# Writing the biases of a four-layer graph kernel into PSUM banks instead of adding them by products

## The chip, the cores and the metric

The kernel runs on one core of one Trainium2 chip. TensorE multiplies and writes only to PSUM, which has eight banks of 512 float32 values in each of 128 partitions. VectorE (DVE in the profile) and ScalarE (ACT) read and write PSUM and SBUF, GpSimd (POOL) works on SBUF, and SyncE (SP) issues the transfers. The metric is the device time in microseconds (us) of one execution. Each engine takes its instructions in the order in which they were written to its queue, and waits on semaphores for the others.

## What is computed

Thirty-two graphs of 512 nodes with 128 features go through four layers. Each layer is preceded by a layer norm and a ReLU, and its result is added to the input. With `h = relu(layernorm(x))`:

```
layer 0: v, q, k = relu(h W + b)              three products, each with a bias
         x += softmax(mask(q k^T, adj)) v
layer 1: dyn = conv1d(last 128 nodes of h) + conv_b
         lw  = lstm(dyn)                      128 steps; all 32 graphs in one batch
                 z = xt w_ih^T + b_ih + hprev w_hh^T + b_hh
         x += sigmoid((A_norm h) lw)          A_norm = D^-1/2 (adj + I) D^-1/2
layer 2: n0 = h; for i in 0..3:
           n(i+1) = tanh([src_agg, self, dst_agg] wu + bu)
           src, dst, self = nodes ws + bs, nodes wd + bd, nodes wn + bn
         x += n4
layer 3: x += prelu(adj (h W^T) + bias)
```

The adjacency is symmetric with a full diagonal. The kernel uses this: it works on one matrix per graph, folds the two aggregations of layer 2 into one, and checks the symmetry as it goes, with a general kernel as the fallback.

## The kernel before

The function `symmetric` doesn't issue instructions as it goes. It collects operations in a `Plan`: each has one or more engines on which it may run, with an estimated duration for each, a rank (lower is more urgent), the buffers it reads and writes, and a function that issues its instructions. `Plan.run` then lays all operations out as a list scheduler would, chooses between ScalarE and VectorE where both are allowed, and calls the issuing functions in order of planned start. A tile framework below it allots the buffers, places the semaphores, and may still change the order on an engine: an instruction whose operands or buffer are not there yet in its own reckoning is passed by one that can go.

There are four groups of operations by rank:

- `pass_1(b)` for each graph b: load x and the last 128 columns of adj, layer norm, transpose (`ln_t`, tile f_xt), the products for keys and queries (f_pq) and values (f_pv), attention for the last 128 nodes (f_sl, f_pol), and the convolution (f_pd) into `seq`. Keys, queries and values go to DRAM.
- `lstm()`: 128 serial steps, rank below 1000, which makes them urgent. A bank `f_z` holds the four gates of four steps for all 32 graphs. At the first of the four the bias (four products of 4 rows, L1069) and the input part (four products, L1073) are written into it, and each step then adds four state products of 32 columns (L1079). A step goes on with a tanh on ScalarE (L1083), three VectorE instructions (L1090 to L1092), a tanh (L1099) and a VectorE product (L1100) which writes `seq` for the next.
- `pass_2(b)`, planned beside the LSTM: attention for the other 384 nodes. It has four score products (f_s, L1120), exponentials and masks, twelve value products (f_po, L1130), the update of x and its statistics.
- `rest(b, end)`: layers 1 to 3. It squares adj with row sums (f_ar), normalises, aggregates (f_pg, L1199), transposes the LSTM output (f_plw, L1206; this waits for the LSTM's last step), makes the gates (f_pl, L1213), checks symmetry (f_aT, L1229), and runs the four sub-layers of layer 2. Each of these has f_py (L1253), a split of f_py into high and low halves by `split` (ScalarE L1147, VectorE L1148), the aggregation into f_pa (L1262), a scaling of f_pa on VectorE (L1265), the own part (L1269) and a tanh (L1273). Layer 3 is f_pf (L1291) and f_pg3 (L1302; the profile drops the 3 and shows f_pg).

Biases that lie along the columns of a bank are added on TensorE. `bias_row` splits a bias row into a high and a low float32r half with four VectorE instructions (`in_parts`), and `add_bias` multiplies a matrix of ones by them as the first product of the bank:

```python
    def add_bias(dst, k, n=NT):
        nc.tensor.matmul(dst, ones_r, bparts[:, k, :].unsqueeze(1).to_broadcast([P, n, P]), start=True, stop=False,
                         skip_group_check=True)
```

This is L838; it is called for f_pv (32 times), f_py (128) and f_pg3 (64). The eight banks are one tag, "mm", of a pool with eight buffers:

```python
    ps = ctx.enter_context(tc.tile_pool(name="f_ps", bufs=BUFS["mm"], space=bass.MemoryType.PSUM))
    def bank(name, shape=(P, 512)):
        return plan.cell(ps, "mm", shape, FP, name)
```

The plan only counts how many are free; which buffer a tile gets is left to the framework.

Of the kernel before, what the change touches and what calls it, by code (L numbers as in the profile page):

```python
# [486 lines left out]
BR_V, BR_3, N_BR = 4, 5, 6  # L487
# [4 lines left out]
class Cell:  # L492


    def __init__(self, pool, tag, shape, dtype, name):
        self.pool, self.tag, self.shape, self.dtype, self.name = pool, tag, shape, dtype, name
        self.real = None
        self.left = 0
        self.free_at = 0.0
        self.parts = {}  # L500

    @property
    def t(self):
        if self.real is None:
            self.real = self.pool.tile(list(self.shape), self.dtype, tag=self.tag, name=self.name)
        return self.real
# [6 lines left out]
class Plan:  # L513
# [4 lines left out]

    HOP, HOP_PE, HOP_URGENT, URGENT = 0.25, 1.2, 0.14, 1000

    def __init__(self, bufs, fifo):
        self.ops = []
        self.bufs = bufs
        self.made = {}
        self.fifo = {t: [] for t in fifo}

    def cell(self, pool, tag, shape, dtype, name):
        c = Cell(pool, tag, shape, dtype, name)
        if tag in self.fifo:
            self.fifo[tag].append(c)  # L530
        return c
# [34 lines left out]
    def run(self):  # L566
# [16 lines left out]
        slots = {t: [0.0] * n for t, n in self.bufs.items()}  # L583
        turn = {t: 0 for t in self.fifo}
        seen = set()
# [40 lines left out]
        while done < len(ops):  # L626
# [33 lines left out]
            for c in o.cells:  # L660
                if c not in seen:
                    seen.add(c)
                    slots[c.tag].remove(min(slots[c.tag]))
# [4 lines left out]
                if c.left == 0:  # L668
                    slots[c.tag].append(c.free_at)
            for n in o.next:  # L670
# [11 lines left out]
def symmetric(ctx, tc, x, adj, weights, cols, rows, lstm_b, prelu_a, out, fail):  # L682
# [25 lines left out]
    ps = ctx.enter_context(tc.tile_pool(name="f_ps", bufs=BUFS["mm"], space=bass.MemoryType.PSUM))  # L708
# [7 lines left out]
    plan = Plan(BUFS, ("ar", "x", "inv", "n0", "n1", "n2", "n3", "a"))  # L716
# [14 lines left out]
    def bank(name, shape=(P, 512)):  # L731
        return plan.cell(ps, "mm", shape, FP, name)
# [33 lines left out]

    def evict(rank, n, dst, src, r, w, relu=False, scale=None):
# [19 lines left out]
    ones_r = const.tile([P, P], FR, name="f_ones_r")  # L787
    nc.vector.memset(f32(ones_r), 1.0)
# [7 lines left out]
    bparts = const.tile([P, N_BR, P], FR, name="f_bparts")  # L796
    lbp = const.tile([4, 4, P], FR, name="f_lbp")
# [10 lines left out]
    lb = const.tile([4, 4, P], FP, name="f_lb")  # L808
    nc.scalar.dma_start(lb[0:2], lstm_b)
    nc.scalar.dma_start(lb[2:4], lstm_b)  # L810
# [4 lines left out]
    mask2 = const.tile([4, 2], FP, name="f_mask2")  # L815
    nc.vector.tensor_add(mask2[:, 0:1], ident[0:4, 0:1], ident[0:4, 1:2])
    nc.vector.tensor_add(mask2[:, 1:2], ident[0:4, 2:3], ident[0:4, 3:4])
    biases = plan.fixed(bparts)
# [4 lines left out]
    def in_parts(rank, n, m, dst, src, masks, r, wr, name):  # L823
        hi = new("gs", (n, m), f"f_bhi_{name}", FR)
        lo = new("gs", (n, m), f"f_blo_{name}")

        def fn():
            nc.vector.tensor_copy(hi.t, src())
            nc.vector.tensor_sub(lo.t, src(), f32(hi.t))
            nc.vector.tensor_scalar_mul(lo.t, lo.t, masks[1])  # L830
            nc.vector.scalar_tensor_tensor(dst, f32(hi.t), masks[0], lo.t, OP.mult, OP.add)
        DVE(rank, 1.2, fn, r, [hi, lo] + wr)

    def bias_row(rank, k, row, r):
        in_parts(rank, P, P, bparts[:, k, :], row, (ident[:, 0:1], ident[:, 1:2]), r, [(biases, k)], k)

    def add_bias(dst, k, n=NT):
        nc.tensor.matmul(dst, ones_r, bparts[:, k, :].unsqueeze(1).to_broadcast([P, n, P]), start=True, stop=False,  # L838
                         skip_group_check=True)
# [5 lines left out]
    bias_row(HEAD, BR_3, lambda: rowb.t[:, R_L3, :], [rowb])  # L845
# [3 lines left out]
    def halves():  # L849
        for q in range(4):  # L850
            half = 1.0 if q == 2 else 0.5
            nc.gpsimd.tensor_scalar_mul(w[:, W_HH + q, :], w[:, W_HH + q, :], 0.5 * half)
            if q != 2:
                nc.gpsimd.tensor_scalar_mul(w[:, W_IH + q, :], w[:, W_IH + q, :], half)
                nc.gpsimd.tensor_scalar_mul(lb[:, q, :], lb[:, q, :], half)
    lbs = plan.fixed(lb)
    POOL(FOLD, 5.0, halves, [], [lbs])
    in_parts(FOLD, 4, 4 * P, flat(lbp), lambda: flat(lb), (mask2[:, 0:1], mask2[:, 1:2]), [lbs], [], "lb")
# [4 lines left out]
    def fold(i):  # L863
# [7 lines left out]
        for c in range(L2_CHUNKS[i]):  # L871
            tp = bank(f"f_wT_{i}_{c}", (P, 3, P))
# [7 lines left out]
            pw = bank(f"f_pw_{i}_{c}", (P, 2, P))  # L880
# [7 lines left out]
        bt_ps = bank(f"f_bT_{i}", (P, 3, P))  # L888
# [7 lines left out]
        pb = bank(f"f_pb_{i}", (P, P))  # L896
# [6 lines left out]
        pc = bank(f"f_pc_{i}", (P, 2))  # L903
# [52 lines left out]
    def ln_t(rank, xn, tag, name):  # L956
# [3 lines left out]
        def fn():  # L960
            for t in range(NT):
                nc.tensor.transpose(tp.t[:, t, :], xn.t[:, t, :], ident)
        PE(rank, 4 * T_TR, fn, [xn], [tp])
        hT = new(tag, (P, N), f"f_hT_{name}")
        evict(rank, N, lambda: hT.t[:, :], lambda: flat(tp.t), [tp], [hT], relu=True)
        return hT
# [6 lines left out]
    def pass_1(b):  # L973
# [6 lines left out]
        hT = ln_t(R, xn, "n0", f"a{b}")  # L980
# [11 lines left out]
        pv = bank(f"f_pv_{b}", (P, NT, P))  # L992

        def values():
            add_bias(pv.t, BR_V)
# [3 lines left out]
        PE(R, t_r(N) + 4 * t_mm(P), values, [hT, (biases, BR_V)], [pv])  # L999
# [12 lines left out]
        def scores():  # L1012
            for t in range(NT):
                nc.tensor.matmul(s.t[:, t, :], kq.t[:, 0, bass.ts(t, P)], kq.t[:, 1, NR:], start=True, stop=True)
# [4 lines left out]
        po = bank(f"f_pol_{b}", (P, P + 1))  # L1019
# [24 lines left out]
        pd = bank(f"f_pd_{b}", (P, P))  # L1044
# [11 lines left out]
    def lstm():  # L1056
# [4 lines left out]
        for t in range(T):  # L1061
            R = t
            k = t % MANY
            if k == 0:
                z = bank(f"f_z_{t}", (P, MANY, 4, B))

                def biases_in(z=z):
# [354 lines left out]
```

## Time and profile before

| | |
|---|---|
| median of 3 runs | 1642.4 us |
| lowest, highest | 1637.87, 1642.55 us |
| the profiled execution | 1644.95 us |
| its span, first to last instruction | 1642.8 us |
| mean granted TensorE clock | 0.972 |
| memory read, written | 117.26 MB, 39.91 MB |

A row of a group shows line, engine, operation, output and inputs, shapes and count; then busy time in us and the mean of one in ns; then the idle time of the engine before them and what ended it. TensorE's records overlap, since a product is recorded until its end while the next has begun: the distance from start to start says what one takes of the engine. A float32 product has two records, a float32r product one. The chain of waits is followed back from the last instruction, and gives start, length and what ran.

### The profile page before, as it was taken

The page shows a single profiled execution, that of the slowest core. Times are in us where ns is not written, and L with a number is a line of the kernel's source. Part 1 is how long each engine was busy: PE and PEld are TensorE (multiplying, and loading weights), DVE is VectorE, ACT ScalarE, POOL GpSimd, SP SyncE. Part 2 cuts the span into 40 slices and gives each one's busy share as a digit, 9 for nine tenths or more (in the row PEclk, how much of TensorE's full clock was granted, in tenths as well). Part 3 has the DMA queues.
Part 4 walks back from the last instruction along what each step waited for, and adds up shares of the span by engine and source line. Part 5 has one row for each costly group of instructions (what it writes and reads, how often), then busy time and mean ns, then how long its engine had stood idle before and what let it go on. Part 6 is the DMA issues. An engine that isn't in the chain of part 4 may idle for free.

```text
span 1642.8 us, 26595 instructions
## 1 busy us (share of the span) xinstructions
PE 1541.6 (94%) x9565; PEld 1253.9 (76%) x9565; DVE 938.4 (57%) x3322; ACT 715.9 (44%) x1700; POOL 322.6 (20%) x624
## 2 busy tenths in 40 slices
PE   4998899999999996999999999999999999999995
PEld 3776678888888885777878887787887787788774
DVE  4665555545554455646746656547656656656543
ACT  3555453323333334645534545435444545454431
POOL 3333331111111112212212212112111212211100
PEclk9999999999999998999999999999999999999997
DMA  7555567454555453101201212112211121111000
GB/s 242 182 187 172 192 203 248 136 165 139 148 152 167 138 147 108 61 33 54 95 14 46 71 39 78 39 39 76 67 39 44 48 65 52 65 39 36 17 13 16
DMA packets 135733, 158.98 MB, mean 97 GB/s; under 512 B 7588, under 2 KB 101924, under 8 KB 135592
## 3 DMA queue, kind: packets, MB, share of 16 engines
q1 hardware_dynamic: 134720, 155.41, 30.1%
q8 instruction: 77, 1.26, 0.3%
q10 hardware_dynamic: 872, 1.78, 0.3%
q14 instruction: 64, 0.52, 0.1%
HBM read 117.26 MB, written 39.91 MB: 96 GB/s over the span
## 4 chain that ended last, share of the span: by engine, by line
PE 42%; DVE 7%; POOL 4%; ACT 4%; DMA 1%; issue 1%; POOLq 0%; ACTq 0%
PE f_pa L1262 11%; PE f_pa L1269 9%; PE f_py L1253 9%; PE f_pg L1302 3%; PE f_pg L1199 2%; ACT f_ar L1163 2%; POOL f_dinv L1173 1%; PE f_pf L1291 1%; DMA f_a<-in_adj_dram 1%; PE f_py L838 1%; PE f_pl L1213 1%; PE f_aT L1229 1%; DVE f_junk L1231 1%; POOL f_rs_c L929 1%; DVE f_pa L1265 1%
## 5 line engine op out<-in xcount | busy, mean ns | idle before, releaser
L1262 PE MATMUL f_pa<-f_ar,f_y 128*128 128x512 f32 x1024 | 272.8, 410 | 5.7 <-DVE f_y L1148 3.0
L1262 PEld LDWEIGHTS f_pa<-f_ar,f_y 128*128 128x128 f32 x1024 | 187.0, 189 | 57.1 <-issue 10.7
L1253 PE MATMUL f_py<-f_wf,f_n 128*128 128x128 f32 x1280 | 174.5, 275 | 1.4 <-ACT f_n L1273 1.3
L1253 PEld LDWEIGHTS f_py<-f_wf,f_n 128*128 128x128 f32 x1280 | 165.2, 192 | 12.9 <-issue 4.3
L1269 PE MATMUL f_pa<-f_n,f_wf 128*128 128x512 f32 x320 | 155.6, 603 | 6.3 <-DVE f_pa L1265 6.2
L1079 PEld LDWEIGHTS f_z<-f_seq,f_w 128*128 128x128 f32 x1016 | 130.9, 200 | 30.7 <-DVE f_seq L1100 26.1
L1079 PE MATMUL f_z<-f_seq,f_w 128*128 128x32 f32 x1016 | 137.6, 280 | 5.5 <-DVE f_seq L1100 3.7
L1273 ACT ACTIVATE f_n<-f_pa,f_bcol 128x512 f32<-128x512 f32 x128 | 87.2, 683 | 107.9 <-PE f_pa L1269 107.8
L1148 DVE TENSOR_TENSOR f_y<-f_py,f_y 128x512 fp32r<-128x512 f32 x128 | 87.2, 685 | 77.0 <-ACT f_y L1147 76.5
L1265 DVE TENSOR_TENSOR f_pa<-f_pa,f_inv 128x512 f32<-128x512 f32 x128 | 88.1, 693 | 57.6 <-PE f_pa L1262 57.4
L1147 ACT CAST f_y<-f_py 128x512 fp32r<-128x512 f32 x128 | 73.6, 580 | 107.1 <-PE f_py L1253 106.5
L1130 PE MATMUL f_po<-f_v,f_e 128*128 128x129 f32 x768 | 119.4, 297 | 0.0
L1130 PEld LDWEIGHTS f_po<-f_v,f_e 128*128 128x128 f32 x768 | 106.9, 207 | 9.0
L940 ACT ACTIVATE f_xn_c<-f_x,f_sh_c,f_rs_c 128x128 f32<-128x128 f32 x127 | 57.0, 489 | 108.7 <-DVE f_sh_c L945 108.4
L1120 PE MATMUL f_s<-f_kq 128*128 128x384 f32 x256 | 103.2, 516 | 0.0
L1083 ACT ACTIVATE f_th<-f_z 128x128 f32<-128x128 f32 x128 | 35.5, 278 | 143.7 <-PE f_z L1079 138.3
L1269 PEld LDWEIGHTS f_pa<-f_n,f_wf 128*128 128x128 f32 x320 | 56.6, 192 | 49.3 <-issue 38.1
L1090 DVE SCALAR_TENSOR_TENSOR f_cu<-f_th,f_c 128x32 f32<-128x32 f32 x127 | 24.4, 192 | 120.9 <-ACT f_th L1083 120.0
L1231 DVE SCALAR_TENSOR_TENSOR f_junk<-f_a,f_aT 128x512 bf16<-128x512 f32 x128 | 86.4, 675 | 4.4 <-PE f_aT L1229 2.4
L1253 PE MATMUL f_py<-f_wf,f_hT_c 128*128 128x128 f32 x512 | 84.4, 277 | 0.7 <-ACT f_hT_c L770 0.7
L1163 ACT ACTIVATE f_ar<-f_a 128x512 fp32r<-128x512 f32 x128 | 79.2, 623 | 6.6 <-DMA f_a<-in_adj_dram 6.6
L1123 ACT ACTIVATE f_e<-f_s 128x384 f32<-128x384 f32 x128 | 62.7, 490 | 38.3 <-PE f_s L1120 36.8
(184 smaller groups left out, 3036.4 us busy)
## 6 DMA issues: line engine op xcount, KB each, us to landing
f_a<-in_adj_dram SPq DMA_DIRECT2D x32, 1024.0 KB, 5.3
f_a<-in_adj_dram SPq DMA_DIRECT2D x32, 768.0 KB, 5.6
f_dkq<-f_kq SPq DMA_DIRECT2D x32, 448.0 KB, 3.7
f_kq<-f_dkq SPq DMA_DIRECT2D x32, 448.0 KB, 4.0
f_dv<-f_v SPq DMA_DIRECT2D x32, 258.0 KB, 3.8
f_v<-f_dv SPq DMA_DIRECT2D x32, 258.0 KB, 2.7
f_x<-in_x_dram SPq DMA_DIRECT2D x32, 256.0 KB, 3.5
f_al<-in_adj_dram SPq DMA_DIRECT2D x32, 256.0 KB, 3.0
```

Of the source, the lines that this page charges most:

```text
L1079: nc.tensor.matmul(z.t[:, k, q, :], w[:, W_HH + q, :], seq[:, t - 1, :], start=False, stop=True, skip_group_check=True)
L1120: PE(R, t_mm(NR), lambda s=s, j=j: nc.tensor.matmul(s.t, kq.t[:, bass.ts(j, P)], kq.t[:, N:], start=True, stop=True), [kq], [s])
L1130: nc.tensor.matmul(po.t[:, t, :], es[j].t[:, bass.ts(t, P)], v.t[:, j, :], start=(j == 0), stop=(j == NT - 1))
L1147: ACT(rank, t_act(N), lambda: nc.scalar.copy(parts.t[:, :, 0, :], src.t), [src], [(parts, 0)])
L1148: DVE(rank, t_dve(N), lambda: nc.vector.tensor_sub(parts.t[:, :, 1, :], src.t, f32(parts.t[:, :, 0, :])), [src, (parts, 0)], [(parts, 1)])
L1163: ACT(R, 0.62, lambda t=t: nc.scalar.activation(ar.t[:, t, :], a.t[:, t, :], AF.Square, accum_out=deg.t[:, t : t + 1]), [a], [(ar, t), (de ...
L1231: DVE(R + 2, 0.7, lambda tp=tp, j=j: nc.vector.scalar_tensor_tensor(junk, a.t[:, j, :], 1.0, flat(tp.t), OP.mult, OP.not_equal, accum_out= ...
L1253: nc.tensor.matmul(py.t[:, j, :], nodes[n].t[:, bass.ts(j, P)], wf[:, W_F[i] + c, 0, :], start=False, stop=(c == nch - 1), skip_group_chec ...
L1262: nc.tensor.matmul(pa.t, parts.t[:, j, k, :], ar.t[:, j, :], start=(k == 0 and j == 0), stop=(k == 1 and j == NT - 1))
L1265: DVE(R, t_dve(N), lambda pa=pa: nc.vector.tensor_mul(pa.t, pa.t, inv_row.t), [inv_row], [pa])
L1269: nc.tensor.matmul(pa.t, wf[:, W_F[i] + c, 1, :], nodes[n].t, start=False, stop=(c == nch - 1), skip_group_check=True)
L1273: ACT(R, 0.5, lambda pa=pa, n=n, i=i: nc.scalar.activation(n.t, pa.t, AF.Tanh, bias=bcol[:, i : i + 1]), [pa], [n])
```

## The change

- No bias is added by a product any more. A bank that takes a bias is declared `filled`, and a new operation `fill` copies the bias row, repeated, into the whole bank, on ScalarE or VectorE as the plan chooses. All products then run with `start=False` and are added to it. For f_z the row `lb_row` holds the four gate biases for all graphs; for f_pg3 it has the bias in the high half's columns and zeros in the low half's.
- Each fill has an operation after which it may start: for f_py the scaling of f_pa of the sub-layer before (or the transpose of the nodes), for f_pv and f_pg3 the transpose before, for f_z the step that was formerly given to the bias products.
- Whether a product adds to what lies in a bank or replaces it depends on marks that earlier products left there. The plan keeps `marked` for each bank: set by a tile declared `whole`, whose products cover the bank under a single start, and cleared by others. `place` picks the bank: among the free ones one whose mark suits the tile, else the longest free. If a fill gets an unmarked bank, a product of zeros over the whole bank is issued first (L859 of the new kernel).
- To leave a bank marked, the four-tile products and transposes now start only at their first tile.
- The pool has one buffer, and the plan's choice is the tag: "mm0" to "mm7".
- The bias rows are copied as they are, instead of being split; the two LSTM biases are transposed together by one product (f_pb8), added, scaled by GpSimd's `halves`, and spread into `lb_row`.

```diff
-    def add_bias(dst, k, n=NT):
-        nc.tensor.matmul(dst, ones_r, bparts[:, k, :].unsqueeze(1).to_broadcast([P, n, P]), start=True, stop=False,
-                         skip_group_check=True)
+    def fill(rank, dst, src, r, c, after):
+
+        def mark():
+            if not c.marked:
+                nc.tensor.matmul(c.t, ident_b, marks, start=True, stop=True)
+
+        def act():
+            mark()
+            nc.scalar.copy(dst(), src)
+
+        def dve():
+            mark()
+            nc.vector.tensor_copy(dst(), src)
+        return plan.op({"ACT": (t_act(N), act), "DVE": (t_dve(N), dve)}, rank, r, [c], after)
...
+        def place(c, s):
+
+            now = [x for x in unused if x[0] <= s + 1e-9] or [min(unused)]
+            at = min(now, key=lambda x: (marked[x[1]] != c.filled, x))
+            unused.remove(at)
+            c.place = at[1]
+            c.marked = marked[c.place]
+            self.sealed += c.filled and not c.marked
+            marked[c.place] = c.whole
+            return at[0]
...
-            self.real = self.pool.tile(list(self.shape), self.dtype, tag=self.tag, name=self.name)
+            tag = self.tag if self.place is None else f"{self.tag}{self.place}"
+            self.real = self.pool.tile(list(self.shape), self.dtype, tag=tag, name=self.name)
...
-    ps = ctx.enter_context(tc.tile_pool(name="f_ps", bufs=BUFS["mm"], space=bass.MemoryType.PSUM))
+    ps = ctx.enter_context(tc.tile_pool(name="f_ps", bufs=1, space=bass.MemoryType.PSUM))
...
-    def bank(name, shape=(P, 512)):
-        return plan.cell(ps, "mm", shape, FP, name)
+    def bank(name, shape=(P, 512), whole=True, filled=False):
+        return plan.cell(ps, "mm", shape, FP, name, whole, filled)
...
+    def turn_tiles(dst, src):
+
+        for t in range(NT):
+            nc.tensor.matmul(dst[:, t, :], src(t), ident, start=(t == 0), stop=True, is_transpose=True, skip_group_check=True)
...
-                z = bank(f"f_z_{t}", (P, MANY, 4, B))
-
-                def biases_in(z=z):
-                    for q in range(4):
-                        nc.tensor.matmul(z.t[:, :, q, :], lbp[:, q, :], ones_r[:4, : MANY * B], start=(q == 0), stop=False,
-                                         skip_group_check=True)
-                PE(R + 2_000, 4 * t_r(P), biases_in, [], [z], after=conv_ops + steps[t - MANY - 1 : t - MANY])
+                z = bank(f"f_z_{t}", (P, MANY, 4, B), filled=True)
+
+                fill(R + 2_000, lambda z=z: z.t.rearrange("p k q b -> p k (q b)"),
+                     lb_row.unsqueeze(1).to_broadcast([P, MANY, 4 * B]), [lbrs], z, conv_ops + steps[t - MANY - 1 : t - MANY])
...
-            py = bank(f"f_py_{b}_{i}", (P, NT, P))
+            py = bank(f"f_py_{b}_{i}", (P, NT, P), filled=True)
+            fill(R, lambda py=py: py.t, bias(i), [(biases, i)], py, [before])
 
             def sent(py=py, i=i, nch=nch):
-                add_bias(py.t, i)
...
-            PE(R, t_r(N) + 4 * nch * t_mm(P), sent, [nodes[n] for n in CHUNKS[i]], [py])
+            PE(R, 4 * nch * t_mm(P), sent, [nodes[n] for n in CHUNKS[i]], [py])
...
-            DVE(R, t_dve(N), lambda pa=pa: nc.vector.tensor_mul(pa.t, pa.t, inv_row.t), [inv_row], [pa])
+            before = DVE(R, t_dve(N), lambda pa=pa: nc.vector.tensor_mul(pa.t, pa.t, inv_row.t), [inv_row], [pa])
...
-            p3 = bank(f"f_pg3_{b}_{k}", (P, 2, 2, P))
+            p3 = bank(f"f_pg3_{b}_{k}", (P, 2, 2, P), filled=True)
+            fill(R, lambda p3=p3: p3.t, bias_3.unsqueeze(1).to_broadcast([P, 2, 2, P]), [b3s], p3, [turned])
```

## Prediction

> **What bounds the kernel now.** I read the page's busy times and slices first, then windows by stage, then the groups kept apart by shape, then two stretches of the timeline.
>
> ```profile
> PE 1541.6 (94%) x9565; PEld 1253.9 (76%) x9565; DVE 938.4 (57%) x3322; ACT 715.9 (44%) x1700; POOL 322.6 (20%) x624
> ...
> 100.00:250.00 150.00, 133.21 (x863) 106.89 (x862) 84.61 (x397) 75.82 (x141) 51.94 (x143) 0.99 0.58 192
> 340.00:640.00 300.00, 287.39 (x1872) 244.52 (x1872) 156.72 (x753) 100.17 (x315) 49.41 (x86) 0.93 0.51 151
> 640.00:800.00 160.00, 150.58 (x908) 121.47 (x908) 99.66 (x294) 80.91 (x192) 31.98 (x53) 0.96 0.18 57
> 800.00:1000.00 200.00, 199.13 (x1231) 161.19 (x1230) 121.87 (x347) 97.83 (x228) 36.06 (x59) 1.00 0.15 49
> ```
>
> Window lines give PE, PEld, DVE, ACT and POOL busy time, then granted clock, DMA share and GB/s. There are three stages: pass 1 (to about 260 us, PE 89% busy in its middle), the LSTM with pass 2 beside it (to 629), and the rest (to the end, PE 97 to 99% busy once it runs). So the rest is bound by TensorE's throughput, and what leaves TensorE there should leave the time. The LSTM stage differs: it is a serial chain, and the timeline shows its period.
>
> ```profile
> 452.56 1.08 PE L1079 MATMUL f_z<-f_seq,f_w 128*128 128x32 f32 x8
> 455.11 1.08 PE L1079 MATMUL f_z<-f_seq,f_w 128*128 128x32 f32 x8
> ...
> 318.00:322.00 4.00, 4.00 (x24) 4.00 (x23) 0.68 (x4) 0.51 (x2) 0.00 (x0) 0.57 0.00 0
> ...
> 320.39 1.75 PE L1079 MATMUL f_z<-f_seq,f_w 128*128 128x32 f32 x8
> ```
>
> An undisturbed step takes 2.55 us (455.11 less 452.56): some 1 us of state products, the remainder ScalarE and VectorE, during which TensorE has 1.6 us for pass 2. At 318 the clock falls to 0.57 and the same eight records take 1.75 us: there TensorE is busy, but with short 32-column products.
>
> **What the skill says.** The Trainium skill, page "PSUM — Partial Sum Buffer", section "The four PSUM rules": VectorE and ScalarE writes leave the has_written bits alone, and a matmul without first_mm adds where the bit is set. So a filled bank works only if an earlier product has set its bits, which is why the plan tells banks apart; nothing in the trace of before shows it. Page "TensorE: Matmul & The Clock Gate", Part 1: a window of about 3.4 us with little activity halves the clock. The trace agrees in size (0.57 at 318, 0.58 in the next 4 us), and shows that "busy" in the record doesn't protect.
>
> **What is removed.** The costs are occupancies, start to start, not the recorded means, which include the pipeline.
>
> ```profile
> L838 PE MATMUL f_py<-f_bparts,f_ones_r 128*128 128x512 f32 x128 | 67.5, 527 | 0.3 <-DVE f_lw L776 0.3
> L838 PE MATMUL f_pv<-f_bparts,f_ones_r 128*128 128x512 f32 x32 | 24.4, 764 | 0.0
> L1069 PE MATMUL f_z<-f_ones_r,f_lbp 4*128 4x128 f32 x128 | 21.9, 284 | 0.0
> L838 PE MATMUL f_pg<-f_bparts,f_ones_r 128*128 128x256 f32 x64 | 20.8, 331 | 0.0
> ...
> 691.12 0.23 PE f_py L838
> ...
> 698.96 2.68 PE f_py L1253 x24
> ```
>
> In the chain of waits (the last two lines: start, length, what) one bias product of 512 columns takes 0.23 us, and 24 records of 128 columns take 2.68, 0.111 each, two to a float32 product. A 256-column product takes 0.12 (sixteen f_pg weight loads in 1.95 us from 1005.61), an LSTM bias product 0.11 to 0.15 (four between 450.99 and 451.58). By stage: rest, 128 x 0.23 + 64 x 0.12 = 37 us; pass 1, 32 x 0.23 = 7 us; LSTM, 128 x 0.13 = 17 us. Together 61 us of TensorE.
>
> **What is added.** In the order of the built program the 256 fills fall 173 to VectorE (95 py, 27 pg, 20 pv, 31 z) and 83 to ScalarE (33, 37, 12, 1). Exactly one marking product is issued, at the head. No row of before copies SBUF to PSUM. From below VectorE's SBUF-to-SBUF 128x512 (f_neg, 484 ns), from above its in-place product in PSUM (f_pa, 693 ns); I take 0.68. ScalarE likewise between 0.49 (its 384-column exp) and 0.68; I take 0.58 (f_y). In the rest that is 122 x 0.68 = 83 us of VectorE over some 960, from 61% to about 70%, and 70 x 0.58 = 41 us of ScalarE. Neither becomes the bound by load. A fill may start as soon as the layer before has its f_pa scaled, a float32 product group (0.86 us or more) and a tanh (0.68) before its consumer, so 0.68 fits. But it waits in an in-order queue for its bank, and behind it there stand the f_y, f_pa and tanh instructions of other batches, for which TensorE waits. Price: 192 fills, each at best free, at worst 0.2 us of TensorE stall, which would give all 37 back. About 5 us of such stalls leaves 32 us gained.
>
> In pass 1, 20 x 0.68 on VectorE (57% busy) are hidden; TensorE idles 11% there, so of the 7 us I count 5. At the head, seven bias splits become single copies, the LSTM bias goes through one transpose on TensorE before GpSimd's halving; both lie under the 16.5 us wait for the row load, and GpSimd's queue waits for the same load as before: nothing. No DMA moves to another queue, though pass 2's come closer together (below). The new start flags and the four-tile transposes have the same count and shape: nothing.
>
> **What is moved.** The diff looks as if the LSTM stage loses 17 us. The order of the built programs says otherwise. Giving each bank its own tag ends the common rotation over eight buffers, and the scheduler now pulls pass 2 forward. Before, pass 2's score (f_s) and value (f_po) products are spread over all the steps; after, the last stands behind the 90th group of state products, and 36 steps follow with little beside them but two batches' f_pg, f_nb and f_aT. I price every step: 0.93 us of states, 0.222 for each f_po or z input product, 0.60 for each f_s (eight records in the 2.37 us from 616.45), at least 2.55 in all. Before: 333 us over 126 intervals; the records of L1083 give 359, so clock dips and VectorE collisions cost 26. After: 264 for the first 90 (2.94 each, TensorE now sets the period) and 92 for the last 36. To the first I add 14 (half of what before lost per step, since a denser TensorE dips less, but VectorE is fuller, the 31 z fills among it). In the last 36 TensorE has 1 us of short products in 2.55, less activity than where before dips; I assume the half clock, 0.7 more a step (1.75 against 1.08): 25. Sum 278 + 117 = 395, 36 us longer. From both sides: with no dip and no added cost 356 (3 us shorter than measured before), with before's loss per step and half clock throughout 264 + 19 + 117 = 400, and more if loads are late: a batch of pass 2 moves 448 + 768 + 258 + 192 + 192 = 1858 KB, now in 264/32 = 8.2 us, which is 225 GB/s on the one SP queue where the page's highest slice has 248.
>
> Against that stands the start of the rest. Its first batches need loads, squares, norms and f_pg after pass 2.
>
> ```profile
> 627.00:640.00 13.00, 3.65 (x27) 3.06 (x25) 5.63 (x26) 6.39 (x20) 7.99 (x16) 0.71 0.31 98
> ...
> 641.40 3.78 PE L1199 MATMUL f_pg<-f_ar,f_xp 128*128 128x512 f32 x8 [7.62 <-ACT f_xp L1182]
> 644.98 0.41 PE L1206 MATMUL f_plw<-f_ident,f_seq 128*128 128x128 f32 x1
> ...
> 656.08 0.30 PE L962 MATMUL f_xt_c<-f_ident,f_xn_c 128*128 128x128 f32 x1 [4.13 <-DVE f_xn_c L937]
> ```
>
> The LSTM ends at 627.1; the first f_xt_c comes 29 us later. After, f_pg of two batches is done before the LSTM ends, and only the piece from f_plw on, 644.98 to 656.08 = 11 us, remains: 18 us gained. What is late next there is the layer norm behind f_pl, on VectorE and GpSimd.
>
> **Sum.** Pass 1 -5, LSTM +36, start of the rest -18, rest -32: -19. The profiled execution took 1644.95 (span 1642.8 and 2 around it), 0.2% over the median of 1642.4; against the median I forecast 1623.
>
> **Rivals.**
> First, the forecast: LSTM later, rest shorter, 1623, chance 0.48.
> Second, the gain comes whole: the clock holds in the thin steps and fills are never late: LSTM +12, start -18, rest -37, pass 1 -6: 1593. For it: the dips of before last only 3 to 7 us each. Against it: they come with far more work beside the chain. Chance 0.16.
> Third, slower: fills hold up the in-order queues in the rest. Place: VectorE, 70% busy, where a fill that waits for a late bank keeps f_y's low half waiting, and through it f_pa. With LSTM +36, start -18 and pass 1 -5 the balance ahead of the rest is +13; so the kernel is slower once the rest gains less than 13, that is from 24/192 = 0.13 us of stall per fill on. At 0.19 the rest gains 1, and the time is 1654. For it: TensorE already waits for VectorE's f_pa and f_y in before. Against it: these waits are only some 10 us in 900, and five batches are in flight. Chance 0.26.
> Fourth, both small: the gain of the rest equals the loss before it, about 1642. Chance 0.10.
> That bias products remain is excluded by the built order, which has one marking product only.
>
> **How the numbers follow.** A measurement of this kernel tells about 0.3%, 5 us, from no change. The first case runs from 1605 to 1637 mostly, with a fringe inside 5 us of no change. Faster: 0.42 of the first and all of the second, 0.58; same: the fourth and a little of the first and third, 0.14; slower 0.28. The range takes the second case's centre and most of the third: 1592 to 1658. The likeliest case's own is 1605 to 1640.
>
> **What would show it.** Right: no L838 or L1069 bias products; f_po ends some 100 us before the LSTM; a granted clock near half in the last 36 steps, at 3.2 us each; from the LSTM's end to the first f_xt_c about 11 us; from there to the end some 32 us less than 1642.8 - 656.1 = 987. Wrong: steps at 2.55 in the thin part (then 1600 or less), first steps well over 3.1 (loads or VectorE late), or TensorE in the rest waiting for fills.

## The result and the profile after

The changed kernel takes 1649.07 us in the median (1646.51 to 1649.17, four runs) beside 1640.13 (1637.34 to 1642.55) for the kernel before: ratio 1.0051, 95% interval 1.0028 to 1.0075. It is slower, by 9 us or half a per cent, where 19 us faster were forecast. The profiled executions lie nearer together (spans 1644.7 and 1642.8), since the one of after is the fastest of its four, and the one of before (1644.95) took longer than the four runs beside it; the stages below are theirs.

The page of after: the first line has busy times, the digits are the granted clock and the memory traffic in 40 slices of 41 us, and the last line is the group of the state products (busy, mean ns, then the idle time before them).

```profile
PE 1490.8 (91%) x9215; PEld 1213.8 (74%) x9215; DVE 1032.0 (63%) x3485; ACT 754.1 (46%) x1774; POOL 317.7 (19%) x624
...
PEclk9999999999999555799999999999999999999997
...
GB/s 248 189 197 177 201 222 256 226 200 222 211 204 139 12 0 1 52 52 52 65 46 71 20 71 65 39 52 65 52 39 71 46 65 52 39 77 14 26 14 16
...
L1122 PE MATMUL f_z<-f_seq,f_w 128*128 128x32 f32 x1016 | 159.0, 306 | 35.1 <-DVE f_seq L1143 34.1
```

TensorE lost 51 us of busy time and the span did not shrink. Three slices in the last third of the LSTM have half the clock, and in the same slices the loads have stopped (12, 0, 1 GB/s). The state products wait 34 us for f_seq; that group had 3.7 before. The windows of after (PE, PEld, DVE, ACT, POOL, then clock, DMA share, GB/s) say the same by stretch:

```profile
260.00:350.00 90.00, 89.77 (x637) 77.42 (x636) 58.71 (x263) 33.66 (x101) 16.83 (x30) 1.00 0.73 220
...
530.00:620.00 90.00, 61.95 (x265) 55.45 (x265) 24.74 (x120) 17.75 (x62) 4.37 (x8) 0.52 0.02 6
...
800.00:1000.00 200.00, 195.49 (x1207) 156.13 (x1207) 143.10 (x388) 106.87 (x246) 37.74 (x61) 1.00 0.18 57
```

First everything is full. Then come 130 us in which VectorE, ScalarE and GpSimd are largely idle, and TensorE is recorded as busy for 62 us of 90, at half the clock. I call the steps of this stretch thin. The timeline shows how it begins, two thin steps, and the start of the rest:

```profile
525.26 0.18 DVE L1143 SCALAR_TENSOR_TENSOR f_seq<-f_th,f_tcn 128x32 f32<-128x32 f32 x1
...
528.37 1.11 PE L795 MATMUL f_nb<-f_ident,f_dinv 128*128 128x128 f32 x4 [3.29 <-POOL f_dinv L1216]
529.28 1.75 PE L1122 MATMUL f_z<-f_seq,f_w 128*128 128x32 f32 x8
...
558.10 1.92 PE L1122 MATMUL f_z<-f_seq,f_w 128*128 128x32 f32 x8 [1.46 <-DVE f_seq L1143]
561.48 1.92 PE L1122 MATMUL f_z<-f_seq,f_w 128*128 128x32 f32 x8 [1.47 <-DVE f_seq L1143]
...
665.73 0.69 PE L1249 MATMUL f_plw<-f_ident,f_seq 128*128 128x128 f32 x2 [0.89 <-DVE f_seq L1143]
676.98 0.69 PE L795 MATMUL f_nb<-f_ident,f_dinv 128*128 128x128 f32 x2 [6.30 <-POOL f_dinv L1216]
```

A thin step takes 3.38 us (561.48 less 558.10), and its eight records 1.92 us, against 2.55 and 1.08 for an undisturbed step before. The first lines show the turn: f_seq is there from 525.44 on, but its state products start at 529.28, because f_nb of the rest stands ahead of them on TensorE and waits 3.29 us for f_dinv, which GpSimd makes.

Four stages are measured in every trace: up to the first f_th; from the first to the last f_th (the LSTM); on to the first f_xt_c; and the rest, to the end of the span. All in us; the ratio is of the medians of several runs, to the runs of before on the same chip.

| kernel | first f_th | LSTM | to f_xt_c | rest | ratio, interval |
|---|---|---|---|---|---|
| before | 262.7 | 363.2 | 30.2 | 986.7 | |
| after | 255.0 | 409.0 | 13.5 | 967.2 | 1.0051, 1.0028 to 1.0075 |
| e1 tags only | 261.1 | 355.8 | 29.5 | 986.6 | 0.9983, 0.9952 to 1.0014 |
| e2 f_z fill only | 265.3 | 400.7 | 12.2 | 997.0 | 1.0202, 1.0146 to 1.0257 |
| e3 f_z by products | 259.8 | 360.8 | 13.5 | 967.2 | 0.9860, 0.9804 to 0.9916 |
| e4 after, plan's order | 258.6 | 385.0 | 13.6 | 967.5 | 0.9882, 0.9829 to 0.9936 |
| e5 f_z fill on ScalarE | 255.7 | 341.5 | 13.6 | 963.4 | 0.9602, 0.9569 to 0.9634 |
| e6 before, plan's order | 260.0 | 377.2 | 41.3 | 985.5 | 1.0139, 1.0090 to 1.0187 |
| e7 e5, rest fills on ScalarE | 256.5 | 342.8 | 11.2 | 960.6 | 0.9562, 0.9527 to 0.9596 |
| e8 e5, rest fills on VectorE | 255.1 | 345.8 | 13.6 | 970.1 | 0.9637, 0.9603 to 0.9670 |
| e9 e4, f_z fill on ScalarE | 256.2 | 374.9 | 13.9 | 964.3 | 0.9779, 0.9734 to 0.9825 |
| e10 e2, fill on ScalarE | 262.7 | 341.6 | 11.2 | 993.0 | 0.9795, 0.9759 to 0.9831 |
| e11 e5, rest fills twice | 257.9 | 343.8 | 13.5 | 970.5 | 0.9664, 0.9629 to 0.9699 |
| e12 after, 6 fillers a step | 258.3 | 407.5 | 13.5 | 967.0 | 1.0048, 1.0033 to 1.0062 |
| e13 after, 18 fillers a step | 258.6 | 393.0 | 13.5 | 964.3 | 0.9952, 0.9934 to 0.9969 |

The stages are of one trace each, and differ by some us where the kernels don't: the first is 255.0 to 258.6 in after, e4, e12 and e13, whose first stage has the same instructions, and the rest is 963.4 to 967.5 in after, e4, e5, e9, e12 and e13, which have the same fills there.

So after against before: -8 up to the LSTM, +46 in it, -17 at the start of the rest, -19.5 in the rest. Against the forecast (-5, +36, -18, -32) two of four terms are clearly off, both to the worse.

### The profile page after: what moved, and what is told of

Its sections match the earlier page's. It is cut to its first block, busy times and chain, and to the rows that moved or that the text cites. A ratio compares the mean times of both kernels' runs of the same rounds, so it can differ in the third digit from the quotient of the medians.

```text
span 1644.7 us, 26237 instructions
## 1 busy us (share of the span) xinstructions
PE 1490.8 (91%) x9215; PEld 1213.8 (74%) x9215; DVE 1032.0 (63%) x3485; ACT 754.1 (46%) x1774; POOL 317.7 (19%) x624
## 3 DMA queue, kind: packets, MB, share of 16 engines
q1 hardware_dynamic: 134720, 155.41, 29.5%
## 4 chain that ended last, share of the span: by engine, by line
PE 38%; DVE 8%; POOL 5%; ACT 5%; DMA 2%; issue 1%; POOLq 0%; ACTq 0%; DVEq 0%; SPq 0%
PE f_pa L1307 10%; PE f_pa L1314 9%; PE f_py L1298 9%; PE f_pg L1347 3%; DMA f_a<-in_adj_dram 2%; PE f_pg L1242 2%; ACT f_ar L1206 2%; POOL f_dinv L1216 2%; PE f_pf L1335 1%; DVE f_junk L1276 1%; PE f_pl L1256 1%; POOL f_rs_c L974 1%; DVE f_pa L1310 1%; POOL f_rs_d L974 1%; PE f_aT L1273 1%
## 5 line engine op out<-in xcount | busy, mean ns | idle before, releaser
L1307 PE MATMUL f_pa<-f_ar,f_y 128*128 128x512 f32 x1024 | 265.5, 405 | 5.6 <-DVE f_y L1191 2.5
L1122 PEld LDWEIGHTS f_z<-f_seq,f_w 128*128 128x128 f32 x1016 | 155.0, 230 | 56.3 <-DVE f_seq L1143 52.6
L1122 PE MATMUL f_z<-f_seq,f_w 128*128 128x32 f32 x1016 | 159.0, 306 | 35.1 <-DVE f_seq L1143 34.1
L1298 PEld LDWEIGHTS f_py<-f_wf,f_n 128*128 128x128 f32 x1280 | 160.3, 192 | 15.0 <-issue 6.6
L1173 PE MATMUL f_po<-f_v,f_e 128*128 128x129 f32 x768 | 108.8, 280 | 0.0
L1310 DVE TENSOR_TENSOR f_pa<-f_pa,f_inv 128x512 f32<-128x512 f32 x128 | 88.4, 691 | 29.6 <-PE f_pa L1307 29.1
L1173 PEld LDWEIGHTS f_po<-f_v,f_e 128*128 128x128 f32 x768 | 97.4, 191 | 8.7
L1163 PE MATMUL f_s<-f_kq 128*128 128x384 f32 x256 | 98.3, 493 | 0.5 <-DVE f_seq L1096 0.5
```

Of the source, the lines that this page charges most:

```text
L1122: nc.tensor.matmul(z.t[:, k, q, :], w[:, W_HH + q, :], seq[:, t - 1, :], start=False, stop=True, skip_group_check=True)
L1163: PE(R, t_mm(NR), lambda s=s, j=j: nc.tensor.matmul(s.t, kq.t[:, bass.ts(j, P)], kq.t[:, N:], start=True, stop=True), [kq], [s])
L1173: nc.tensor.matmul(po.t[:, t, :], es[j].t[:, bass.ts(t, P)], v.t[:, j, :], start=(j == 0), stop=(j == NT - 1))
L1298: nc.tensor.matmul(py.t[:, j, :], nodes[n].t[:, bass.ts(j, P)], wf[:, W_F[i] + c, 0, :], start=False, stop=(c == nch - 1), skip_group_chec ...
L1307: nc.tensor.matmul(pa.t, parts.t[:, j, k, :], ar.t[:, j, :], start=(k == 0 and j == 0), stop=(k == 1 and j == NT - 1))
L1310: before = DVE(R, t_dve(N), lambda pa=pa: nc.vector.tensor_mul(pa.t, pa.t, inv_row.t), [inv_row], [pa])
```

## The experiments

### What makes pass 2 run ahead: e1, e2, e3

e1 is the kernel before with the plan's choice of banks alone; all bias products stay.

```diff
-            self.real = self.pool.tile(list(self.shape), self.dtype, tag=self.tag, name=self.name)
+            tag = self.tag if self.place is None else f"{self.tag}{self.place}"
+            self.real = self.pool.tile(list(self.shape), self.dtype, tag=tag, name=self.name)
...
-    ps = ctx.enter_context(tc.tile_pool(name="f_ps", bufs=BUFS["mm"], space=bass.MemoryType.PSUM))
+    ps = ctx.enter_context(tc.tile_pool(name="f_ps", bufs=1, space=bass.MemoryType.PSUM))
```

> The kernel before with one part of the change alone: the plan chooses the bank of each tile and every bank has a tag of its own; all bias products stay. Theory A (the prediction's: the separate tags let pass 2 run ahead of the LSTM): LSTM stage from first to last f_th near 400 us instead of 363, a granted clock near one half in its last third, 1660 us or more. Theory B (the fill of f_z does it, not the tags): LSTM stage 363 us and the time within 0.3% of before, 1640. In the built order the last product of pass 2 stands behind step 126, as in before, which speaks for B.

Measured: 0.9983, no difference. The LSTM takes 355.8 us and the last f_po starts at 623.4, 6.5 us after the last f_th: pass 2 isn't moved. The tags alone are not the cause.

e2 is the changed kernel with the bias products put back for f_pv, f_py and f_pg3, so that the fill of f_z is the only one left. e3 is the opposite: only f_z has its bias products again.

```diff
-            fill(R, lambda py=py: py.t, bias(i), [(biases, i)], py, [before])
+                add_bias(py.t, i)
...
-                fill(R + 2_000, lambda z=z: z.t.rearrange("p k q b -> p k (q b)"),
+                PE(R + 2_000, 4 * t_r(P), biases_in, [], [z], after=conv_ops + steps[t - MANY - 1 : t - MANY])
```

(The first pair of lines belongs to e2, the second to e3.)

> The changed kernel with bias products put back for f_pv, f_py and f_pg3: only f_z is filled. Theory A (tags): no different from e1. Theory B (the fill of f_z): pass 2 ends by step 96 in the built order, so the LSTM stage is 395 to 410 us with a thin, half-clocked end, and nothing is gained in the rest beyond an earlier start: 1655 to 1670 us. Theory C (the LSTM stage of the changed kernel is late because VectorE is full with all fills): LSTM stage near 363, 1640.

> The changed kernel with one part undone: f_z gets its bias by four products as before; all other fills and the banks stay. Theory B: pass 2 is spread over all steps again, LSTM stage about 363 us and ending near 620; the rest from the LSTM's end takes some 29 us to the first f_xt_c and then 967 as in the changed kernel: about 1616 us. Theory C (rest gains nothing of its own, what it shows is work done early beside the LSTM): 1635 to 1640.

Measured: e2 1675.44 us, LSTM 400.7; e3 1616.93, LSTM 360.8. Of the parts tried here the loss in the LSTM follows the fill of f_z alone, and the fills of the other tiles are a gain.

Three figures don't fit theory B. The total of e2 is above its band of 1655 to 1670, with a rest 10 us longer than that of before. The first f_xt_c of e3 comes 13.5 us after the LSTM and not 29, though pass 2 ends only 14 us ahead of the LSTM (last f_po 606.3, last f_th 620.6): a short lead is enough for the early start. And that e3's median lies on the 1616 us expected is luck, since the sum expected has the 29. The trace of e3 is the fastest of its four runs (1603.14 to 1622.78); where the slower ones spend their time no trace shows.

### Order or delay: e4, e6, e9

e4 is the changed kernel with the LSTM's and pass 2's products held in the plan's own order on TensorE; e6 does so to the kernel before, and e9 has e4's order with the fills of f_z on ScalarE.

```diff
+    def in_order(*a, **k):
+        return tc.keep_in_program_order(nc.tensor.matmul(*a, **k))
...
-                        nc.tensor.matmul(z.t[:, k, q, :], w[:, W_HH + q, :], seq[:, t - 1, :], start=False, stop=True,
+                        in_order(z.t[:, k, q, :], w[:, W_HH + q, :], seq[:, t - 1, :], start=False, stop=True,
```

> The changed kernel with one edit: the products of the LSTM and of pass 2 are issued on TensorE in the plan's own order, so nothing of pass 2 runs ahead. If the order alone lengthens the LSTM stage: about 350 to 363 us with the clock at 0.9 or more, the LSTM's end near 610, total 1600 to 1612 us. Rival: a fixed order makes TensorE wait at its head for pass 2's operands, and f_z's fill on VectorE is what delays the chain: LSTM stage 380 or more, 1630 or more.

> The kernel before with the products of the LSTM and of pass 2 kept in the plan's own order on TensorE, bias products and all: the control for the run in which the changed kernel was kept in that order (LSTM stage 385 us, TensorE idle 0.34 us a step, waiting for f_seq). Theory C1 (the plan's own order is by itself less dense than the scheduler's, and that is why pinning won back only 24 of the 46 us): LSTM stage 385 to 400 us instead of 363, total 1660 to 1680. Theory C2 (the fills on VectorE still hold up the recurrence when the order is pinned): without fills the pinned stage is as short as before, 355 to 368 us, total 1632 to 1645.

> The changed kernel with both edits: LSTM and pass 2 kept in the plan's order on TensorE, and the fills of f_z on ScalarE. Its pair is the run with the plan's order and the fills on VectorE (LSTM stage 385 us, total 1624). With the order held, only the fill's place differs. Theory G (a fill of 0.69 us between f_cv and f_c delays the recurrence by itself, order apart): LSTM stage 355 to 368 us, total 1595 to 1607. Theory H (only the scheduler's order matters, and the plan's order costs the rest): LSTM stage 380 to 388 us, total 1619 to 1628.

Measured: e4 1623.78 us, LSTM 385.0; e6 1666.8, LSTM 377.2; e9 1607.32, LSTM 374.9. Holding the order takes 24 of the 46 us back; e4's LSTM lies in its rival's band, its total between the two. It isn't a good order: it costs the kernel before 14 us in the LSTM and another 11 before f_xt_c. C1 and C2 each have a part: e6's LSTM lies between their bands, its total in C1's. So have G and H: e9's LSTM lies between their bands, its total at the edge of G's. With the order held, moving the fill from VectorE to ScalarE is worth 10 us of the LSTM and 16 in all. TensorE's wait for the recurrence, in the stretch from 262 to 600, shows it (us in total, times, longest), first for e4, then for e9:

```profile
PE f_z L793 <- DVE f_seq L1146: 36.8, 58, 0.9
```

```profile
PE f_z L793 <- DVE f_seq L1149: 27.1, 60, 0.9
```

### The engine of one fill: e5, e10

e5 is the changed kernel with the 32 fills of f_z on ScalarE. e10 does the same to e2.

```diff
-        return plan.op({"ACT": (t_act(N), act), "DVE": (t_dve(N), dve)}, rank, r, [c], after)
+        ways = {"ACT": (t_act(N), act), "DVE": (t_dve(N), dve)}
+        if on:
+            ways = {on: ways[on]}
+        return plan.op(ways, rank, r, [c], after)
```

> The changed kernel with one thing altered: the 32 fills of f_z go to ScalarE alone (in the changed kernel 31 of 32 went to VectorE, 0.69 us each, between f_cv and f_c of the recurrence). In its order on TensorE the last products of pass 2 come after step 118, not 90. Theory C (the loss in the LSTM stage is that pass 2 runs ahead and leaves thin steps at half the clock, and it runs ahead because the fill stands on VectorE's side of the recurrence): LSTM stage 350 to 360 us instead of 409, clock at full speed until near its end, total 1600 to 1616. Theory D (a fill in the recurrence costs its own time on whichever engine, and the order only follows): each of 32 fills still delays f_th or f_tcn by 0.3 to 0.6 us on top of a packed TensorE, LSTM stage above 380 us, total 1630 or more.

> Bias products put back for f_pv, f_py and f_pg3, the fill of f_z alone is left, and it stands on ScalarE: the pair of the run where it stood on VectorE (ratio 1.020, LSTM stage 401 us, rest 997). Theory C: LSTM stage 340 to 350, rest 985 to 1000 (no fills there), total 1605 to 1622; and the difference to e5, 30 us of rest and 7 of pass 1, is what the other fills are worth. Theory D': without the other edits the ScalarE fill doesn't repair it, LSTM stage above 380, total above 1650.

Measured: e5 1579.98 us, 4.0% faster than before; e10 1609.1 instead of e2's 1675.44. Theory C holds; e10 lies in its bands, and e5 is better than expected: its LSTM takes 341.5 us, 22 less than before. Thirty-one copies of 0.69 us, 21 us in all, moved to the other engine, are worth 67 us of the LSTM (409.0 to 341.5; from e2 to e10 it is 59 us of the LSTM and 66 in all). The timelines of VectorE, ScalarE and TensorE around one fill show the direct part. After, with the fill on VectorE:

```profile
407.75 0.28 ACT L1126 ACTIVATE f_th<-f_z 128x128 f32<-128x128 f32 x1 [0.32 <-PE f_z L1122]
408.06 0.19 DVE L1133 SCALAR_TENSOR_TENSOR f_cu<-f_th,f_c 128x32 f32<-128x32 f32 x1 [0.17 <-ACT f_th L1126]
408.16 0.18 DVE L1134 SCALAR_TENSOR_TENSOR f_cv<-f_th 128x32 f32<-128x32 f32 x1
408.27 0.69 DVE L867 COPY f_z<-f_lb_row 128x512 f32<-128x512 f32 x1
...
408.86 0.18 DVE L1135 SCALAR_TENSOR_TENSOR f_c<-f_cu,f_cv 128x32 f32<-128x32 f32 x1
```

e5, with the fill on ScalarE:

```profile
401.73 0.28 ACT L1129 ACTIVATE f_th<-f_z 128x128 f32<-128x128 f32 x1 [1.39 <-PE f_z L1125]
...
402.04 0.59 ACT L863 COPY f_z<-f_lb_row 128x512 f32<-128x512 f32 x1
402.04 0.19 DVE L1136 SCALAR_TENSOR_TENSOR f_cu<-f_th,f_c 128x32 f32<-128x32 f32 x1 [1.48 <-ACT f_th L1129]
402.15 0.18 DVE L1137 SCALAR_TENSOR_TENSOR f_cv<-f_th 128x32 f32<-128x32 f32 x1
402.36 0.19 DVE L1138 SCALAR_TENSOR_TENSOR f_c<-f_cu,f_cv 128x32 f32<-128x32 f32 x1
...
402.59 0.23 ACT L1145 ACTIVATE f_tcn<-f_c 128x32 f32<-128x32 f32 x1
```

On VectorE the copy stands between f_cv and f_c, and f_c starts 0.70 us after f_cv instead of 0.21. On ScalarE it fills the pause in which VectorE works, and f_tcn follows f_c after 0.23 us. This direct part was 10 us with the order held (e4 to e9), so by this estimate the larger part of the 67 goes with the order: the last f_po starts at 524.7 in after and at 568.7 in e5. The windows of e5 have no thin stretch before the end:

```profile
260.00:350.00 90.00, 89.56 (x623) 76.72 (x623) 53.57 (x255) 37.68 (x112) 16.20 (x27) 1.00 0.68 207
350.00:440.00 90.00, 89.61 (x621) 76.50 (x619) 54.58 (x266) 38.15 (x115) 15.95 (x27) 1.00 0.61 182
...
530.00:620.00 90.00, 71.86 (x449) 61.90 (x448) 51.96 (x222) 39.27 (x120) 18.77 (x35) 0.83 0.29 93
```

From 260 to 350 TensorE is as busy in after (89.77 us of 90) as in e5 (89.56): after puts more of pass 2 into each of these steps, and the time is lost in the thin ones, where pass 2 has run out. Why the framework runs pass 2 ahead when the copy stands on VectorE was not traced.

The 22 us gained against before are more than the 17 of bias products removed. The clock goes with it: 1.00 in the first two of these windows, where the kernel before has 0.94 and 0.91:

```profile
260.00:350.00 90.00, 87.73 (x575) 74.48 (x574) 46.11 (x228) 28.14 (x89) 12.43 (x21) 0.94 0.57 166
350.00:440.00 90.00, 88.91 (x566) 75.67 (x565) 45.28 (x215) 28.00 (x89) 12.51 (x21) 0.91 0.50 146
```

So it is in the other traces looked at. While pass 2 runs beside the LSTM, the mean clock is 0.95 to 0.98 with the bias products of f_z on TensorE (e1, e3 and e6, from 262 to 600) and 1.00 without them (after and e2 from 262 to 520, e4 to 600, e9 to 590). It is not that TensorE was busier without them. With the plan's order it was less busy; e6 (bias products), then e4 (fills):

```profile
262.00:600.00 338.00, 312.71 (x2028) 253.63 (x2029) 167.38 (x799) 102.05 (x325) 41.94 (x75) 0.95 0.47 142
```

```profile
262.00:600.00 338.00, 300.89 (x2056) 245.15 (x2054) 199.02 (x895) 111.25 (x349) 44.81 (x87) 1.00 0.52 161
```

What it is about these products (their four rows, or the gaps around them) no run separates.

### What a fill costs in the rest: e7, e8, e11

All three start from e5. In e7 the 192 fills of f_py and f_pg3 are all on ScalarE, in e8 all on VectorE (e5: 70 and 122), and in e11 each is executed twice.

```diff
-            fill(R, lambda py=py: py.t, bias(i), [(biases, i)], py, [before])
+            fill(R, lambda py=py: py.t, bias(i), [(biases, i)], py, [before], on="ACT")
...
-            nc.vector.tensor_copy(dst(), src)
+            for _ in range(times):
+                nc.vector.tensor_copy(dst(), src)
```

(The first pair is e7, with "DVE" e8; the second is e11.)

> As e5, and in the rest all 192 fills (f_py 128, f_pg 64) on ScalarE; the plan put 70 there and 122 on VectorE. ScalarE gains 122 x 0.59 = 72 us, VectorE loses 122 x 0.69 = 84 us of 967. Theory E (VectorE, 67% busy in the rest, holds f_pa and f_y back behind fills, which is why 35 us less TensorE work gave only 20): rest 950 to 962 us, 5 to 17 faster than e5. Theory F (fills are hidden on either engine; the idle time of TensorE comes from the chain f_n, f_pa, f_xn_d that is there anyway): within 4 us of e5.

> As e5, and in the rest all 192 fills on VectorE: 70 x 0.69 = 48 us more there, 70 x 0.59 = 41 us less on ScalarE. Theory E: f_pa and f_y come later, rest 972 to 990 us, 5 to 20 slower than e5. Theory F: within 4 us of e5.

> As e5 (rest 963 us), but each of the 192 fills of the rest is executed twice on its engine: 122 more fills of 0.69 us on VectorE (84 us), 70 of 0.59 us on ScalarE (41 us). Theory F (fills hidden): at most 5 us slower than e5. Theory E (each fill on VectorE delays f_pa or f_y behind it): moving 70 fills to VectorE cost 7 us of rest, 0.1 us each, so 122 more there cost 12 us and total 1588 to 1598. The third rival of the prediction (stall of 0.13 us or more per fill): 25 us or more slower, above 1604.

Measured against e5's rest of 963.4: e7 960.6, e8 970.1, e11 970.5. In the times, e7 is 1572.69 us, e8 1586.68, e11 1588.0, e5 1579.98; the intervals of neighbours overlap, those of e7 and e8 do not. So both theories have a part: 70 fills moved to VectorE cost 6.7 us, 0.10 each (theory E); 122 moved away from it gain 2.8 (theory F, and inside the 4 us by which this stage differs between traces); 192 executed again cost 7.1, 0.04 each, and bring the total to the lower edge of E's band. The fills are mostly hidden, and below the 0.13 us each from which the third rival would have decided.

The windows of the whole rest, one line each for before, e10 (bias products in the rest) and e5 (fills), split the gain:

```profile
656.08:1642.80 986.72, 947.39 (x5720) 759.50 (x5720) 584.09 (x1669) 459.33 (x1052) 172.68 (x276) 0.99 0.15 48
```

```profile
615.50:1608.50 993.00, 948.94 (x5718) 761.28 (x5718) 583.47 (x1659) 455.21 (x1040) 171.98 (x276) 0.98 0.15 46
```

```profile
610.80:1574.20 963.40, 910.73 (x5527) 726.38 (x5525) 650.71 (x1779) 488.35 (x1107) 165.39 (x272) 0.99 0.15 47
```

From e10 to e5 TensorE loses 38.2 us of work and gains 8.6 of idle time (44.1 to 52.7): the fills are worth 29.6 us. From before to e10 the start is 19 us earlier, but the rest is 6.3 longer; e2 shows the same, 18 and 10.3. That the one causes the other is not shown: at the first f_xt_c the same numbers of f_pg, f_aT and f_pl records (16, 32 and 16) lie behind in all three.

### The clock in the thin steps: e12, e13

The changed kernel, with products by a tile of zeros added to f_z's bank ahead of the state products of steps 94 and later: 6 a step in e12, 18 in e13.

```diff
                 def states(z=z, t=t, k=k):
+                    if t >= 94:
+                        for _ in range(18):
+                            nc.tensor.matmul(z.t[:, k, :, :], ident_b, marks[:, :P], start=False, stop=False,
+                                             skip_group_check=True)
```

> The changed kernel with 6 products by a tile of zeros, added to the bank of f_z ahead of the state products of every step from 94 on, where TensorE waits 1.47 us for f_seq; one such product of 128x128 bf16 takes 0.073 us at full clock by the trace. 6 take 0.4 us at full clock and 0.9 at half, so they hold nothing up. Theory K (the thin steps are long because the share of TensorE's time in which it works falls too low and the clock is halved): 6 are too few, the clock stays near half, steps 3.38 us, LSTM stage 405 to 412, total 1642 to 1655. Theory L (the step is set by the recurrence and hand-over, the clock is not what lengthens it): the same.

> As e12 with 18 such products a step: 1.3 us at full clock, inside the 1.47 us of waiting. Theory K: the clock goes back to full, the eight state records take 1.08 instead of 1.92 us, steps 2.55 to 2.65 us instead of 3.38, some 31 of them: LSTM stage 380 to 388 us, total 1620 to 1630. Theory L: no gain, or slower by the added work (2.6 us a step at half clock against 1.47 of waiting: LSTM stage 430 or more, total 1665 or more).

Measured: e12 1648.21 us, as after; e13 1631.95. Theory K holds for both, with a smaller gain in e13 than its bands (LSTM 393.0, not 380 to 388; total above 1620 to 1630). The timeline of e13 shows why:

```profile
602.85 1.17 PE L1123 MATMUL f_z<-f_marks,f_ident_b 128*128 128x128 bf16 x18 [0.20 <-ACT f_th L1130]
...
603.95 1.08 PE L1126 MATMUL f_z<-f_seq,f_w 128*128 128x32 f32 x8
...
606.50 1.08 PE L1126 MATMUL f_z<-f_seq,f_w 128*128 128x32 f32 x8 [1.47 <-DVE f_seq L1147]
607.94 2.08 PE L1123 MATMUL f_z<-f_marks,f_ident_b 128*128 128x128 bf16 x18 [0.36 <-ACT f_th L1130]
609.81 1.86 PE L1126 MATMUL f_z<-f_seq,f_w 128*128 128x32 f32 x8
```

With 18 fillers the states take 1.08 us and the step is 2.55 again: added work made it shorter. Ahead of 606.50 there is no filler, TensorE waits 1.47 us, and from then on the clock is halved, fillers and states take 2.08 and 1.86 us, and a step with fillers is 4.09 to the end of the LSTM. All 612 fillers (34 steps of 18) are in the trace, but the framework didn't leave them in their places: those of a bank's first step don't depend on f_seq and ran behind the bank's input products, the first of them at 498.29. So one step in four had no filler of its own. In the earlier of these steps input products or f_pg stood in that place; at 606.50 nothing did. The windows of e13 on both sides:

```profile
595.00:605.00 10.00, 9.26 (x99) 7.81 (x97) 2.78 (x14) 2.33 (x8) 0.00 (x0) 1.00 0.01 2
...
625.00:635.00 10.00, 9.27 (x66) 9.05 (x63) 1.36 (x8) 1.01 (x4) 0.00 (x0) 0.50 0.00 0
```

## Why the prediction was wrong

Pass 2 runs ahead, the last steps are thin and have half the clock, the rest starts early and gains: the mechanism forecast is what the traces show. Two terms of its sum were mis-sized, and one cause was wrong.

**The steps that failed.** The first is in "What is moved", the price of the last 36 steps: 92 us, and 25 for the half clock, 117 in all. On the prediction's count, which leaves out the first interval (2.16 us), they took 132.9. The second is the "Sum": it adds -18 for the start of the rest and -32 for the rest as if each came whole. The rest gained 19.5.

**LSTM, +36 forecast, +46 measured.** On the same count the first 90 steps were put at 278 us and took 274.0. The 14 us in this term are called half of what before lost per step; half of 26 us over 126 steps is 9 us for 90. Measured were 10 us over the 264 of pure work, 4 of them at the turn. The clock held at 1.00, but the reason given, that a denser TensorE dips less, is not borne out: e4 was less busy than e6 and had the higher clock. The dip shown at 318 doesn't prove it either: at half the clock the same work fills more of the time, so part of the 4.00 us busy of 4 comes of the dip. In the 3.4 us ahead (315.1 to 318.5) TensorE was busy for 3.05 us.

In the last 36 steps three things cost more. Two steps at the turn, where f_pg and f_nb of the rest come between, took 11.0 us instead of 6.5; the prediction saw these products there and gave them no price. The thin steps took 3.38 instead of 3.25. And up to 4.56 came every fourth step while there are fills and input products; the fills were priced in the lump for the first 90 steps only. The half clock was foreseen, and e13 confirms its part: with it lifted for about half of the thin stretch the LSTM was 16 us shorter.

The Trainium skill, page "TensorE: Matmul & The Clock Gate", section "Why this matters for your kernels", advises no idle gaps above some 3 us. That fits the turn: the clock was 1.00 from 524.2 to 527.6, while TensorE waited 3.29 us for f_dinv, and 0.51 in the 3.4 us after. It is not enough in the thin steps: there gaps of 1.47 us in steps of 3.38 keep the half clock.

**The cause of the order.** "Giving each bank its own tag ends the common rotation over eight buffers, and the scheduler now pulls pass 2 forward." That pass 2 runs ahead was read off the built program and was right; its cause was read off the diff and was wrong. With the tags alone (e1) nothing moves; with one fill on VectorE (e2) all of it comes, and with that fill on ScalarE (e5, e10) most of it goes. No figure of the forecast hung on this, but the remedy did: the 31 fills of f_z were listed as VectorE's, and that ScalarE pauses at this place of the step was not asked.

**Start of the rest, -18 forecast, -17 measured**; from f_plw to f_xt_c 11.7 us (665.73 to 677.46) where 11 were forecast.

**Rest, -32 forecast, -19.5 measured.** The mis-sized term is not the fills, which are worth 29.6 us (e10 to e5; e2 to after 29.8). The start and the rest were added as if independent: in e10 and e2, where the start is early and the rest has no fills, the rest is 6 and 10 us longer than before, and 29.8 less 10.3 is the 19.5. Why it is longer stays open.

**Pass 1, -5 forecast, -8 measured**, which is no miss beside the 4 us by which this stage differs between traces.

**The rivals.** The second is refuted (the clock didn't hold in the thin steps). The third's mechanism, a fill that holds up VectorE's queue, was real, but mainly in the LSTM and not in its place. The fourth, that gain and loss cancel, came nearest in the sum: with terms of -8, +46, -17 and -19.5 it is +2 for the profiled pair, though the terms are not small. That 1649 lies inside the range of 1592 to 1658 is luck: the range reached so far up for the third rival.

## What to carry to other kernels

Work taken off the busiest engine has to be put somewhere: ask of each new instruction which serial chain its engine is part of, and put it on the engine that pauses in that chain (here ScalarE, idle while VectorE works on the cell). When a scheduler decides the order, change one edit at a time and look at the order, since a copy of 0.69 us, 31 times, moved a whole stage. A price for thin steps needs the work that will come between them, and what that work waits for. The best version of this study, e7, has the change as it is, with all fills of f_z, f_py and f_pg3 on ScalarE: 1572.69 us, ratio 0.9562, interval 0.9527 to 0.9596.

## What the runs showed of the hardware

- TensorE can be recorded as busy for 9.3 us of 10 at full clock and at half clock alike (e13, 595 to 605 and 625 to 635). In the second window its work was the 18 fillers and eight state records a step of the first (which had some f_pg and f_aT too), only slower; after one step with 1.47 us of waiting the clock did not come back for the 45 us left of the LSTM. The Trainium skill, page "TensorE: Matmul & The Clock Gate", Part 1, says that sustained busy time of one window of about 3.4 us restores it; in these 45 us it did not, so the record's "busy" isn't that measure.
- With the bias products of f_z on TensorE the clock dipped beside pass 2 (0.95 in e6, busy 312.71 us of 338); without them it held (1.00 in e4, busy 300.89 of 338).
- 18 products of zeros, 1.17 us (0.065 each; 0.073 was expected), in a wait of 1.47 us shortened a step from 3.38 to 2.55 us (e13); 6 of them changed nothing (e12).
- A 128x512 float32 copy from SBUF to PSUM took 0.69 us on VectorE (after) and 0.59 on ScalarE (e5).
